# Renumbered weight slots and new step lists in a graph transformer and GAT kernel

## The chip, the cores and the metric

The kernel runs on one core of a Trainium2 chip. A core has a matrix engine (PE, with its weight loader PEld), a vector engine (DVE), a scalar engine (ACT), a general engine (POOL) and a queue engine (SP) that here issues nearly all DMAs. Each engine works through its own instructions in the order in which the program gives them; between engines semaphores order the work. The metric is the time of the whole kernel on the device in microseconds (us), lower being better.

## The reference, cut to what matters

The input is `x` of 128 graphs x 128 nodes x 512 features, and a weighted adjacency `adj` of 128 x 128 x 128. Two layers follow each other, each with a layer norm and a relu in front and a residual sum behind:

```python
h = jnp.maximum(_layernorm(x, axis=-1), 0.0)
q, k, v = (h @ W.T + b for W, b in ((Wq, bq), (Wk, bk), (Wv, bv)))   # 8 heads of 64
scores = q @ k.T * SCALE * (adj + adj)        # per head
x = x + softmax(scores) @ v @ Wo.T + bo
h = jnp.maximum(_layernorm(x, axis=-1), 0.0)
Wh = h @ W
e = leaky_relu(Wh @ a[:512] + (Wh @ a[512:]).T, 0.2)
x = x + elu(softmax(where(adj > 0.5, e, -9e15), axis=1) @ Wh)
```

Everything is float32.

## The kernel before, in words

**Units of work.** Two graphs are a pair (64 pairs, `p`), two pairs are a group (32 groups, `g`). A group's query, key and value projections are not computed as plain products. The 4 x 4 blocks of the three weight matrices and the 4 blocks of tokens and features go through a fast matrix multiplication scheme: 26 block products (`TERMS`), 17 sums of input blocks per group (`FORMS`), and 35 sums of weight blocks that are computed once (`WSUMS`). The other two large products, of the attention context with `Wo` and of the gathered features with `W`, take 7 block products per pair (`PRODUCTS`).

**Steps and names.** The kernel is cut into small steps, each with a short name and a pair:

- `Tk` makes form `k` on POOL (L281). `Qn` multiplies term `n` for queries and keys (L296, two matmuls that the profile records as four passes of 256 columns), `Vn` for values (L305, four passes of 128 columns). `An` and `Bn` take the accumulated sum out of PSUM after the term: the first for a block is a copy by ACT (L320, L333), the others are additions by DVE (L322, L335). Terms of one chain go on accumulating in the same bank, so the next product of the chain has to wait until the take has read it.
- `sca`, `scb` are the attention scores of the pair's two graphs (PE L373), `at..` weighs them with the adjacency (DVE L380), `mx.` takes the maxima (DVE L387), `ex..` the exponentials (ACT L392), `rc..` the reciprocals (DVE L396), `nm..` scales (ACT L401).
- `fl.` transposes 32 x 32 blocks (DVE L408), `bl.` writes them to DRAM (SP L412), `pl.` reads them back into transposed places (SP L418, four DMAs), and `pc.` multiplies with the values (PE L441). `pe.` and `cs0` to `cs3` prepare the context for the seven products (ACT L448, DVE L190 to L196).
- `o0` to `o6` are the seven products with `Wo` (PE L348), `od..` adds them to `x` (DVE L455). `w0` to `w6` are those with `W` (PE L348), `zc.` copies and `wd.` adds their results (ACT L548, DVE L552). `g0`, `g1` gather (PE L534).
- `lx`, `l0`, `lT`, `la`, `lt`, `f0` are loads on SP; `t0`, `t1` (DVE L204, L205) take layer norm statistics of the pair five further on, `pp` (POOL L212) their power, `hn` normalises (DVE L229), `tp` transposes on PE (L236), `ev` keeps the transposed rows (ACT L239): the first four pairs are normalised in this way.
- `L0` to `L3` load four raw weight blocks each into `w_sb` (SP L160, 768 KB each), `W0` to `W34` are the sums of weight blocks (DVE L166, L169).

**Order.** Nothing is scheduled at run time, and PE, DVE, ACT, POOL and SP each take their share of the steps in the order of three written lists. `HEAD` (730 entries `step@pair`) is run once. `ORDER` (341 entries `step:lag`, acting on pair `2g - lag`) is run for `g` from 2 to 28, so 27 times; each turn does one group's worth of every step. `TAIL` (1051 entries, the number counted back from the last pair) ends the work. A name that stands where no such step exists any more is passed over. All PSUM tiles come in turn from one pool of 8 banks (`ps1`).

**Buffers near the change.** `w_sb` has 28 slots of three 128 x 128 blocks. Slots 0 to 15 take the raw blocks, and many of the sums overwrite raw blocks that are used up. The host lays `wT` out so that it matches the slots.

Of the kernel before, what the change touches and what calls it, by code (L numbers as in the profile page):

```python
# [13 lines left out]
P = 128  # L14
# [10 lines left out]
def kernel(  # L25
# [16 lines left out]
    nc = tc.nc  # L42
    B, S, E = x.shape
    C = E // P
# [22 lines left out]
    def sums(text):  # L67
# [7 lines left out]
        1,8,7,13- 0,10,18,10- 1,9,19,03- 0,11,0,00- 1,1,20,01+ 0,2,16,. 1,13,5,11+ 0,0,21,03- 1,12,6,12- 0,0,1,02-  # L75
        1,14,14,02- 0,18,24,00+ 0,3,26,01+ 3,20,15,03+ 2,21,22,02- 3,19,25,13+ 2,22,23,12- 3,16,9,11- 2,6,10,.
        3,17,27,01- 2,4,2,13+ 3,15,4,00- 2,4,3,10- 3,23,12,10- 2,24,8,12+ 2,7,13,11-
# [5 lines left out]
        7=15-7 16=8-4 17=15-11 18=17-16 0=1-0 19=7-18 19=19-0 9=9n11 11=9n15 5=5-11 20=5-7 6=6n5 5=14n6 21=15-3  # L83
        21=21-0 22=10n17 23=1n2 24=23-22 25=24-15 3=3+1 1=25+3 14=14n22 24=12n24 26=13-12 27=11-12 2=7+2 2=3+2 4=11-4
        3=3n19 17=8-17 12=17-12 8=19+20 8=5-8 11=5+11 13=11-13
# [55 lines left out]
    w_sb = const.tile([P, SLOTS, 3, P], F32, name="w3")  # L141
# [16 lines left out]
    def load_blocks(n):  # L158

        nc.sync.dma_start(w_sb[:, n : C * C : C], wT[:, n : C * C : C])  # L160
# [464 lines left out]
    def listed(text, mark):  # L625
# [3 lines left out]
        lx@1 t0@-4 t1@-4 lx@0 t0@-5 pp@1 hn1@1 tp1@1 ev1@1 hn0@1 L0@0 L3@0 W2@0 W0@0 t1@-5 pp@0 W1@0 lx@2 t1@-3 tp0@1  # L629
        ev0@1 T0@-2 hn1@0 tp1@0 ev1@0 T4@-2 T8@-2 L1@0 W7@0 hn0@0 W4@0 W3@0 V0@-2 B0@-2 tp0@0 ev0@0 W8@0 W5@0 W13@0  # L630
        W9@0 Q0@-2 A0@-2 W6@0 T1@-2 Q2@-2 T2@-2 V1@-2 l0@-2 t0@-2 L2@0 t1@-2 V2@-2 T3@-2 B1@-2 V3@-2 B3@-2 B2@-2
        W14@0 Lu@0 W10@0 pp@3 hn0@3 Q1@-2 A1@-2 la@-1 W16@0 W11@0 V5@-2 V7@-2 B7@-2 Q3@-2 A2@-2 Q4@-2 V4@-2 A3@-2
        W15@0 hn1@3 W17@0 W19@0 W12@0 W18@0 W21@0 B4@-2 W20@0 W29@0 W31@0 Q5@-2 Q7@-2 A7@-2 W22@0 Lo1@0 W24@0 A4@-2
        T5@-2 Q6@-2 V6@-2 tp1@3 A6@-2 Q8@-2 Q9@-2 B6@-2 V8@-2 A8@-2 W25@0 V9@-2 Lc@0 l0@0 t1@0 T7@-2 t0@-3 t0@0 T9@-2
        T10@-2 A9@-2 Q11@-2 A11@-2 ev1@3 B9@-2 W23@0 V11@-2 tp0@3 T6@-2 Q10@-2 B8@-2 ev0@3 W26@0 W28@0 T11@-2 T12@-2
        Q13@-2 s0@0 A13@-2 A10@-2 V10@-2 Q12@-2 W27@0 W33@0 Q15@-2 A15@-2 A12@-2 B10@-2 T13@-2 V14@-2 Q14@-2 V13@-2
        B13@-2 B11@-2 A14@-2 Q17@-2 A17@-2 B14@-2 pp@2 V15@-2 V12@-2 B15@-2 T16@-2 T14@-2 Q16@-2 A16@-2 hn1@2 V16@-2
        B16@-2 Q19@-2 A19@-2 Q18@-2 Q20@-2 l0@-1 t1@-1 Q21@-2 V18@-2 V17@-2 A20@-2 hn0@2 A21@-2 W30@0 B17@-2 Q22@-2
        A22@-2 B12@-2 W32@0 T0@0 t0@-1 Q0@0 T15@-2 V20@-2 Q23@-2 A23@-2 sca@0 Lo0@0 Wo0@0 Lw0@0 scb@0 ata1@0 ata0@0
        Q24@-2 A0@0 tp0@2 ev0@2 V0@0 B20@-2 V22@-2 mxa@0 exa3@0 exa2@0 W34@0 tp1@2 l0@2 la@0 B22@-2 V24@-2 V19@-2  # L640
# [299 lines left out]
```

## Time and profile before

| what | value |
|---|---|
| time of the kernel, median of three runs | 2327.14 us (2325.97 to 2329.51) |
| the profiled execution's own time | 2323.18 us |
| its span, first to last instruction | 2321.4 us |
| mean granted PE clock | 0.997 |
| PE busy, share of the span | 2291.4 us, 99% |
| DVE busy | 2099.9 us, 90% |
| ACT busy | 1460.3 us, 63% |
| POOL busy | 972.8 us, 42% |
| 16 DMA engines, mean busy share | about half; 0.93 in the first 20 us |
| PE busy in the first 200 us | 184.99 us |
| PE busy in the last 200 us | 187.31 us |

One turn of `ORDER` takes 70.95 us in the middle of the run: the same burst of score products begins at 1033.61 and again at 1104.55. So the 27 turns make up 1915.7 us of the span; the remaining 406 us belong to `HEAD` and `TAIL`. In the middle of the run a stretch of 73 us has 72.93 us of busy PE and about 66.4 us of busy DVE. A busy PE is not yet a PE at its fastest, because the profile models where a matmul ends: what counts is the distance from one start to the next. The profiler's times of one execution are used below for single instructions, the median of the runs for the kernel.

### The profile page before, as it was taken

Reading aid. Unit: us, or ns where it says so; the run is one execution under the profiler, and the core shown is the slowest. Engines: PE = TensorE matmul, PEld = TensorE weight load, DVE = VectorE, ACT = ScalarE, POOL = GpSimd, SP = SyncE. Lnnn points to the kernel's source line nnn. Section 1 sums busy time; section 2 is a strip of 40 time slices with the busy share of each in tenths; the row PEclk is TensorE's granted clock in tenths of the full one; section 3 lists DMA queues with packets and bytes.
Section 4 is the critical chain, followed back from the end, with each engine's and each line's share of the span. In section 5 each row is a group of like instructions: output and inputs, shape, how many; then the busy total and the mean of one; then the engine's idle time right before and its main releaser. Section 6 shows DMA issues by size and latency. Waiting matters only on the chain.

```text
span 2321.4 us, 45352 instructions
## 1 busy us (share of the span) xinstructions
PE 2291.4 (99%) x15444; PEld 2037.5 (88%) x15444; DVE 2099.9 (90%) x4620; ACT 1460.3 (63%) x4942; POOL 972.8 (42%) x1112
## 2 busy tenths in 40 slices
PE   8999999999999999999999999999999999999998
PEld 6888888888888888888888888888888888888986
DVE  8998999998999999999989999999999899999897
ACT  2566666666665766666666657666666666566665
POOL 3634443443443444434434434444344344344211
PEclk9999999999999999999999999999999999999999
DMA  4544654545544545545455455454454554544432
GB/s 164 148 119 119 157 137 135 148 120 145 151 124 138 144 121 157 135 137 148 120 145 150 124 139 139 125 157 134 137 143 126 145 150 124 139 125 124 119 121 89
DMA packets 267471, 314.60 MB, mean 136 GB/s; under 512 B 23656, under 2 KB 193640, under 8 KB 267240
## 3 DMA queue, kind: packets, MB, share of 16 engines
q1 hardware_dynamic: 263736, 311.57, 48.6%
q8 instruction: 123, 2.02, 0.4%
q0 software_dynamic: 1920, 0.13, 0.1%
q14 instruction: 108, 0.88, 0.1%
q10 hardware_dynamic: 1584, 0.01, 0.0%
HBM read 210.77 MB, written 100.85 MB: 134 GB/s over the span
## 4 chain that ended last, share of the span: by engine, by line
PE 92%; DVE 4%; DMA 1%; ACT 1%; issue 1%; POOL 1%; SPq 0%; POOLq 0%; DVEq 0%; ACTq 0%
PE acc_q L296 30%; PE row_a L348 24%; PE acc_v L305 14%; PE row_c L348 9%; PE pc L441 5%; PE sc L373 5%; PE pg L534 5%; DVE st L204 1%; DVE w L169 1%; DVE qk L322 1%; ACT z L548 1%; DMA aT<-blocks 0%; DMA w<-in_wT 0%; DVE junk L478 0%; DVE x L455 0%
## 5 line engine op out<-in xcount | busy, mean ns | idle before, releaser
L296 PE MATMUL acc_q<-tf,w 128*128 128x256 f32 x2176 | 550.1, 384 | 2.2 <-DVE w L169 1.6
L281 POOL TENSOR_TENSOR tf<-hA,tf 128x256 f32<-128x256 f32 x288 | 225.0, 786 | 660.7 <-PE acc_v L305 642.4
L296 PEld LDWEIGHTS acc_q<-tf,w 128*128 128x128 f32 x2176 | 393.0, 190 | 63.0 <-ACT qk L320 8.4
L392 ACT ACTIVATE at<-at,nmx 128x128 f32<-128x128 f32 x1024 | 397.5, 391 | 35.8 <-DVE nmx L387 33.7
L322 DVE TENSOR_TENSOR qk<-qk,acc_q 128x512 f32<-128x512 f32 x512 | 341.8, 678 | 31.6 <-PE acc_q L296 28.4
L305 PEld LDWEIGHTS acc_v<-w,tf 128*128 128x128 f32 x2176 | 312.4, 191 | 24.7 <-POOL tf L281 2.1
L348 PE MATMUL row_a<-w,gT 128*128 128x256 f32 x1272 | 327.7, 384 | 4.3 <-ACT gT L540 0.7
L401 ACT ACTIVATE at<-at,rs 128x128 f32<-128x128 f32 x1024 | 329.1, 396 | 1.2 <-DVE rs L396 1.2
L305 PE MATMUL acc_v<-w,tf 128*128 128x128 f32 x2176 | 321.6, 275 | 1.9 <-POOL tf L281 1.8
L348 PE MATMUL row_a<-wo,cxT 128*128 128x256 f32 x1272 | 320.9, 382 | 0.8 <-DVE x L455 0.5
L296 PE MATMUL acc_q<-hA,w 128*128 128x256 f32 x1152 | 295.3, 380 | 0.0
L348 PEld LDWEIGHTS row_a<-w,gT 128*128 128x128 f32 x1272 | 233.6, 190 | 42.3 <-ACT z L548 8.5
L348 PEld LDWEIGHTS row_a<-wo,cxT 128*128 128x128 f32 x1272 | 231.5, 190 | 37.3 <-DVE x L455 10.0
L335 DVE TENSOR_TENSOR v<-v,acc_v 128x256 f32<-128x256 f32 x512 | 206.2, 408 | 33.1 <-PE acc_v L305 31.7
L296 PEld LDWEIGHTS acc_q<-hA,w 128*128 128x128 f32 x1152 | 208.7, 190 | 27.3 <-DVE qk L322 4.3
L380 DVE SCALAR_TENSOR_TENSOR at<-sc,adj 128x512 f32<-128x512 f32 x256 | 166.1, 681 | 44.3 <-PE sc L373 44.2
L478 DVE SCALAR_TENSOR_TENSOR junk<-h,u 128x512 f32<-128x512 f32 x256 | 200.2, 782 | 3.4 <-ACT h L471 1.0
L281 POOL TENSOR_TENSOR tf<-hA 128x256 f32<-128x256 f32 x128 | 93.4, 741 | 257.8 <-PE acc_v L305 194.0
L548 ACT COPY z<-row_a 128x256 f32<-128x256 f32 x256 | 93.3, 364 | 163.3 <-PE row_a L348 158.6
L392 ACT ACTIVATION_READ_ACCUMULATOR at<-at,nmx 128x1 f32 x1024 | 194.0, 189 | 0.0
L320 ACT ACTIVATE qk<-acc_q,bq 128x256 f32<-128x256 f32 x256 | 120.1, 469 | 113.7 <-PE acc_q L296 113.6
L269 POOL TENSOR_TENSOR x<-x,c 128x512 f32<-128x512 f32 x128 | 174.9, 1386 | 22.5 <-DMA x<-in_x 9.5
(97 smaller groups left out, 4162.8 us busy)
## 6 DMA issues: line engine op xcount, KB each, us to landing
blocks<-tr SPq DMA_DIRECT2D x128, 512.0 KB, 5.5
aT<-blocks SPq DMA_DIRECT2D x512, 128.0 KB, 3.5
x<-in_x SPq DMA_DIRECT2D x123, 512.0 KB, 4.0
out<-x SPq DMA_DIRECT2D x63, 512.0 KB, 3.3
hA<-in_xT SPq DMA_DIRECT2D x120, 256.0 KB, 4.1
mr<-rows SPq DMA_DIRECT2D x60, 256.0 KB, 3.2
adj<-in_adj SPq DMA_DIRECT2D x64, 128.0 KB, 2.2
adjT<-in_adjT SPq DMA_DIRECT2D x64, 128.0 KB, 5.5
```

The lines of the kernel that those rows point to most:

```text
L269: nc.gpsimd.tensor_tensor(xs[p][:, i, :], xs[p][:, i, :], c_sb, OP.add)
L281: eng.tensor_tensor(forms[g, 2 * C + k], form(g, a), form(g, b), OP.add if op == "+" else OP.subtract)
L296: nc.tensor.matmul(acc[:, i, :], w_sb[:, slot, i, :], form(g, f), start=fresh and i == 0, stop=True, skip_group_check=True)
L305: nc.tensor.matmul(acc[:, i, :], form(g, f)[:, i * P : (i + 1) * P], w_sb[:, slot, 2, :], start=fresh and i == 0, stop=True, skip_group_ch ...
L320: nc.scalar.activation(d[:, i, :], acc[:, i, :], AF.Identity, bias=bias[:, j : j + 1], scale=float(sign))
L322: nc.vector.tensor_tensor(d, d, acc, OP.add if sign > 0 else OP.subtract)
L335: nc.vector.tensor_tensor(d, d, acc, OP.add if sign > 0 else OP.subtract)
L348: nc.tensor.matmul(acc, left[:, la, c, :], w[:, wb, c, :], start=first, stop=c == 1, skip_group_check=True)
L380: nc.vector.scalar_tensor_tensor(ats[b][0][:, k * C : (k + 1) * C, :], scs[b][k], QSCALE, adjs[p][:, i : i + 1, :].to_broadcast([P, C, S]) ...
L392: nc.scalar.activation(at[:, j, :], at[:, j, :], AF.Exp, bias=nmx[:, j : j + 1], accum_out=sums[:, j : j + 1])
L401: nc.scalar.activation(at[:, j, :], at[:, j, :], AF.Copy, scale=rs[:, j : j + 1])
L478: nc.vector.scalar_tensor_tensor(junk, h2[:, i, :], 1.0, u_sb[:, k, :], op0=OP.mult, op1=OP.mult, accum_out=ws[:, i, 1:2] if k else src_sb ...
```

## The change

The change renumbers slots and rewrites lists; no instruction's shape and no arithmetic is changed.

- `wT` is laid out on the host by output block and then by input block, where it was the other way round, so that the four blocks that one `load_blocks` brings stand next to each other, in DRAM as well as in `w_sb`. Each of the four loads then moves 6,144 bytes per partition in one run where it moved four runs of 1,536 bytes. `TERMS` and `WSUMS` name the new slot numbers; the sums and products are the same.
- `HEAD`, `ORDER` and `TAIL` hold the same steps in another order. The cut between the three lists is moved too (710, 341 and 1071 entries): a few steps that ended `HEAD` now begin `ORDER`.

The core of the diff, with the beginning of `HEAD`, and of `ORDER` the lines that matter later:

```diff
     TERMS = list(terms("""
-        1,8,7,13- 0,10,18,10- 1,9,19,03- 0,11,0,00- 1,1,20,01+ 0,2,16,. 1,13,5,11+ 0,0,21,03- 1,12,6,12- 0,0,1,02-
+        1,8,13,13- 0,10,18,10- 1,9,19,03- 0,11,0,00- 1,1,20,01+ 0,2,16,. 1,13,5,11+ 0,0,21,03- 1,12,9,12- 0,0,4,02-
...
     WSUMS = list(sums("""
-        7=15-7 16=8-4 17=15-11 18=17-16 0=1-0 19=7-18 19=19-0 9=9n11 11=9n15 5=5-11 20=5-7 6=6n5 5=14n6 21=15-3
+        13=15-13 16=2-1 17=15-14 18=17-16 0=4-0 19=13-18 19=19-0 6=6n14 14=6n15 5=5-14 20=5-13 9=9n5 5=11n9 21=15-12
...
-        nc.sync.dma_start(w_sb[:, n : C * C : C], wT[:, n : C * C : C])
+        nc.sync.dma_start(w_sb[:, n * C : (n + 1) * C], wT[:, n * C : (n + 1) * C])
...
     HEAD = """
-        lx@1 t0@-4 t1@-4 lx@0 t0@-5 pp@1 hn1@1 tp1@1 ev1@1 hn0@1 L0@0 L3@0 W2@0 W0@0 t1@-5 pp@0 W1@0 lx@2 t1@-3 tp0@1
-        ev0@1 T0@-2 hn1@0 tp1@0 ev1@0 T4@-2 T8@-2 L1@0 W7@0 hn0@0 W4@0 W3@0 V0@-2 B0@-2 tp0@0 ev0@0 W8@0 W5@0 W13@0
-        W9@0 Q0@-2 A0@-2 W6@0 T1@-2 Q2@-2 T2@-2 V1@-2 l0@-2 t0@-2 L2@0 t1@-2 V2@-2 T3@-2 B1@-2 V3@-2 B3@-2 B2@-2
...
+        lx@1 t0@-4 L3@0 t1@-4 lx@0 t0@-5 L1@0 pp@1 hn0@1 hn1@1 W2@0 t1@-5 W13@0 tp0@1 ev0@1 W7@0 W0@0 tp1@1 L0@0
+        ev1@1 pp@0 hn1@0 tp1@0 ev1@0 W1@0 T0@-2 V0@-2 hn0@0 tp0@0 W8@0 W3@0 W4@0 T4@-2 B0@-2 ev0@0 W5@0 T1@-2 T2@-2
+        W9@0 Q0@-2 A0@-2 W6@0 V2@-2 T3@-2 B2@-2 Q2@-2 V1@-2 B1@-2 Q1@-2 l0@-2 t1@-2 t0@-2 pp@3 A2@-2 T5@-2 V3@-2 lx@2
...
     ORDER = """
...
-        sca:0 scb:0 pea:1 peb:1 pw:2 nm:2 h20:2 h21:2 ata0:0 w0:3 zc0:3 ata1:0 V25:2 cs0:1 mxa:0 exa1:0 exa0:0 d10:2
-        d00:2 atb1:0 px:2 rca0:0 atb0:0 w2:3 T1:0 Q2:0 zc2:3 T3:0 T2:0 f0:0 Q1:0 V1:0 exa2:0 T7:0 t0:-2 nma0:0 w4:3
-        mxb:0 A2:0 nma1:0 exb0:0 o0:1 B25:2 zc4:3 lx:1 sh:1 o1:1 od0:1 w3:3 V0:0 exb1:0 cs1:1 o2:1 B1:0 t1:-2 lT:0
-        exa3:0 d11:2 T5:0 Q4:0 exb3:0 od1:1 wd4c:3 rcb0:0 od2:1 w1:3 cs2:1 rca1:0 lT:-1 cs3:1 wd1:3 pd:2 d01:2 pv:2
-        hd0:0 hd1:0 exb2:0 rcb1:0 A1:0 wm:2 l0:-1 nma3:0 nma2:0 o4:1 o3:1 w6:3 od4:1 V3:0 Q3:0 f0:-1 fla:0 bla:0
...
-        V5:0 la:-2 lt:0 blb:0 od6:1 B2:0 V4:0 pr:2 m1:2 B4:0 A6:0 e1:2 V7:0 s0:-2 T6:0 T9:0 B7:0 od5:1 Q7:0 A7:0
-        hd0:-1 Q8:0 st0:1 Q9:0 sw:2 A9:0 V6:0 pla:0 V9:0 B9:0 g1:2 st1:1 hd1:-1 zc5:3 fa:3 T10:0 V11:0 g0:2 B6:0 V8:0
-        B11:0 Q11:0 A11:0 ge1:2 ez:3 gs0:2 B8:0 V10:0 B10:0 T11:0 T12:0 fb:3 A8:0 Q10:0 plb:0 Q13:0 A13:0 so:3 lx:0
-        gs2:2 pw:1 nm:1 h21:1 h20:1 V12:0 A10:0 gs1:2 B12:0 Q12:0 A12:0 Q15:0 A15:0 pca:0 sca:-1 scb:-1 pcb:0 ata1:-1
...
+        pr:3 A20:2 V18:2 V20:2 B20:2 V21:2 B21:2 od4:2 wd6:4 m1:3 o3:2 Q22:2 Q0:0 fa:4 o5:2 A22:2 e1:3 sw:3 T16:2
+        V22:2 B22:2 Q24:2 ez:4 A0:0 T15:2 Q23:2 T8:0 od4c:2 o6:2 V23:2 V24:2 T1:0 pla:1 od1:2 A24:2 od5:2 fb:4 g1:3
+        ge1:3 g0:3 plb:1 ge0:3 od6:2 B24:2 st0:2 st1:2 Q25:2 A25:2 gs2:3 B23:2 gs0:3 so:4 V25:2 B25:2 A23:2 pca:1
+        pcb:1 sca:0 scb:0 T2:0 pw:2 nm:2 peb:1 cs0:1 h21:2 ata0:0 ata1:0 h20:2 d10:2 mxa:0 pea:1 d00:2 Q2:0 atb1:0
+        atb0:0 A2:0 Q1:0 V1:0 o0:1 o1:1 exa2:0 A1:0 w0:3 w1:3 lt:1 lT:0 V0:0 T3:0 T5:0 px:2 cs1:1 lt:2 cs2:1 Q4:0
+        Q3:0 mxb:0 lx:1 sh:1 od0:1 o2:1 exa1:0 exa3:0 f0:0 hd0:0 T7:0 rca1:0 t0:-2 exa0:0 exb3:0 zc0:3 B0:0 V2:0
+        t1:-2 B1:0 V3:0 rca0:0 od1:1 A3:0 Q5:0 nma0:0 od2:1 cs3:1 o4:1 Q7:0 o3:1 hd1:0 B2:0 pd:2 pv:2 B3:0 wd1:3
+        nma1:0 gs1:3 w2:3 d01:2 od4:1 l0:-1 la:-2 exb2:0 A4:0 gs3:3 wm:2 d11:2 rcb1:0 nma2:0 zc2:3 V4:0 nma3:0 fla:0
+        lT:-1 t1:-1 od4c:1 w3:3 f0:-1 o5:1 w4:3 V5:0 V7:0 exb0:0 B4:0 V6:0 pr:2 nmb2:0 m1:2 od5:1 A7:0 hd0:-1 B7:0
+        exb1:0 rcb0:0 T9:0 T6:0 st0:1 B6:0 bla:0 nmb3:0 zc4:3 wd4c:3 Q6:0 o6:1 od6:1 nmb1:0 nmb0:0 A6:0 T10:0 Q9:0
+        V9:0 V8:0 flb:0 e1:2 A9:0 st1:1 w6:3 wd6:3 blb:0 Q8:0 hd1:-1 w5:3 sw:2 B8:0 B9:0 V11:0 A8:0 pla:0 Q11:0 V10:0
+        T11:0 T12:0 zc5:3 fa:3 A11:0 B11:0 plb:0 g0:2 g1:2 ez:3 ge1:2 fb:3 so:3 pw:1 nm:1 B10:0 V13:0 ge0:2 h21:1
+        Q13:0 A13:0 gs0:2 V12:0 gs2:2 Q12:0 Q15:0 gs1:2 Q10:0 B12:0 h20:1 d10:1 A10:0 A12:0 gs3:2 d00:1 pca:0 sca:-1
+        scb:-1 pcb:0 peb:0 ata1:-1 pea:0 ata0:-1 B13:0 px:1 pd:1 mxa:-1 atb1:-1 w0:2 zc0:2 atb0:-1 exa1:-1 T14:0
+        T13:0 V14:0 exa3:-1 exa2:-1 exa0:-1 V15:0 B15:0 A15:0 mxb:-1 exb2:-1 w1:2 exb0:-1 o0:0 lx:0 exb3:-1 cs0:0
...
-            np.transpose(np.reshape(np.stack([L0_gnn_Wq, L0_gnn_Wk, L0_gnn_Wv]), (3, 4, P, 4, P)), (4, 3, 1, 0, 2)),
+            np.transpose(np.reshape(np.stack([L0_gnn_Wq, L0_gnn_Wk, L0_gnn_Wv]), (3, 4, P, 4, P)), (4, 1, 3, 0, 2)),
```

## The prediction

> **What bounds the kernel now.** I read first the busy shares and slices of the page, then the chain of work that ended last over one turn of the loop, then the order of PE's instructions in time around the breaks of that chain, then the waits by engine, and last the first 24 us.
>
> ```profile
> PE 2291.4 (99%) x15444; PEld 2037.5 (88%) x15444; DVE 2099.9 (90%) x4620; ACT 1460.3 (63%) x4942; POOL 972.8 (42%) x1112
> PE   8999999999999999999999999999999999999998
> ```
>
> PE is busy throughout, but its ends are modelled. The chain gives its pace, in start us, us, what:
>
> ```profile
> 1031.71 1.90 PE pc L441 x32
> 1033.61 1.99 PE sc L373 x32
> 1040.47 2.59 PE row_a L348 x12
> 1055.78 1.34 PE acc_v L305 x12
> 1068.84 1.02 PE pc L441 x16
> ```
>
> A pass of 256 columns costs 2.59/12 = 0.216 us, one of 128 columns 1.34/12 = 0.112. A turn has 26 Q steps and 14 products with Wo and W per pair, (26 + 28) x 4 = 216 wide passes, 46.6 us; 104 passes of V and 32 of g, 136 narrow ones, 15.2; two bursts of scores, 3.98; contexts 1.90 + 2 x 1.02 = 3.94. Sum 69.7 us. Going in and out of a burst of scores and contexts costs about 0.1 us each time, 0.4 in a turn. A turn takes 70.95. So about 0.8 us of a turn is PE standing, and it is here:
>
> ```profile
> 1036.49 0.61 PE L305 MATMUL acc_v<-w,hA 128*128 128x128 f32 x4
> 1037.17 1.13 PE L348 MATMUL row_a<-w,gT 128*128 128x256 f32 x4
> ...
> 1056.95 1.03 PE L296 MATMUL acc_q<-hA,w 128*128 128x256 f32 x4
> 1057.88 1.13 PE L296 MATMUL acc_q<-tf,w 128*128 128x256 f32 x4
> ```
>
> These are PE's rows: start, length, line, operation. V25's four passes begin at 1036.49 and take 4 x 0.112; w2 begins at 1037.17, 0.24 late. And a group of four wide passes that runs through has 1.03 us, one that follows a wait has 1.13: each wait costs 0.10 us on top of itself. The waits of the whole run name the producers (total us, times, longest):
>
> ```profile
> PEld row_a L348 <- DVE x L455: 10.0, 31, 0.9
> PEld row_a L348 <- ACT z L548: 8.5, 30, 0.9
> PEld acc_q L296 <- ACT qk L320: 8.4, 29, 0.3
> PEld acc_q L296 <- DVE qk L322: 5.1, 29, 0.5
> ```
>
> About 30 times means once in each turn. From the rows in time the five places are, late plus 0.10: w2 after zc0 0.24 + 0.10 (1037.17); o4 after od2 0.05 + 0.10 (1046.85); Q8 after A6 0.06 + 0.10 (1057.88); Q9 after A7 0.02 (1058.84); Q10 after A8 0.06 + 0.10 (1064.67). Sum 0.83, which is the 0.8 (two of the five are shown above, the others read in the same rows). The loop is thus 98.8% PE at its own pace; DVE with 66.4 of 73 us has room.
>
> The head is different. PE in the first 24 us, and the chain there:
>
> ```profile
> 8.17 1.11 PE L236 MATMUL pt<-ident,hn 128*128 128x128 f32 x8 [1.35 <-DVE hn L229]
> 15.28 1.11 PE L236 MATMUL pt<-ident,hn 128*128 128x128 f32 x4 [6.00 <-DVE hn L229]
> 18.05 1.91 PE L296 MATMUL acc_q<-tf,w 128*128 128x256 f32 x4
> 21.57 1.10 PE L296 MATMUL acc_q<-tf,w 128*128 128x256 f32 x4 [1.61 <-DVE w L169]
> ```
>
> ```profile
> 4.40 6.77 DMA w<-in_wT
> 11.19 1.03 DVE w L169 x2
> ```
>
> PE stands for 6 us until pair 0 is normalised on DVE, which itself stands 2.6 us for a load of weights and then sums weights. PE is busy for 185.0 of the first 200 us and 187.3 of the last 200.
>
> **What the Trainium skill says.** "TensorE: Matmul & The Clock Gate", Architectural detail: PE can pull weight loads ahead of running matmuls, while ACT and DVE are strict first in, first out. The trace agrees: without a wait the loads are hidden (0.216 a pass, while a load lasts 0.19), and a take of PSUM is late when something long stands before it on its engine. The page has no price for a restart; the 0.10 is this trace's. Same page, What's actually happening: after about 3.4 us idle PE runs at half clock, and as long again until it recovers. The trace agrees: after the 6 us gap Q0's four passes take 1.91 us, later ones 1.10. "DMA: Bandwidth & Descriptors", Why small descriptors are slow: about 3 cycles a packet beside 32 bytes a cycle. For four runs of 1,536 bytes against one of 6,144 that is 204 against 195 cycles, 4%.
>
> **The change, part by part.** Durations come from the profiled execution (2323.18 us; span 2321.4, and 1.8 around it). The median of the runs is 2327.14, 4.0 more, which I carry over unchanged.
>
> *Contiguous loads.* Same four DMAs, same bytes. At 324 GB/s (the first 20 us) 768 KB take 2.4 us; 4% of it, an estimate from that page, is 0.1 us a load. Bounds: 0 to 0.5 us for all four; I take 0.2, inside the head's figure below. Slot numbers cost nothing: same instructions, same shapes.
>
> *ORDER, the five waits.* Each goes if enough PE work stands between the take's source and the product that waits. (Q, o or w = 0.86 us, V = 0.45, g = 0.89.)
> - w2 behind zc0: between w0 and w2 stood V25 (0.45), and it was 0.24 late, so 0.69 is needed. For lag 3 twelve steps now stand there. For lag 2 the waiting one is now w1, with V14 and V15, 0.90, between: margin 0.2.
> - Q9 behind A7: only Q8 stood between Q7 and Q9; now eleven steps.
> - Q8 behind A6: A6 stood in ACT's queue behind pr (two instructions) and nmb; now two nmb steps, four scalings of about 0.3 us by their spacing, and o6, Q9, V9, V8, w6 (3.5 us) cover them.
> - Q10 behind A8: A8 stood behind ge1 and ez, and Q10 next to it. Now g0, g1, V13, Q13, V12, Q12, Q15 and more lie between, over 5 us.
> - o4 behind od2: Q4 and w1 (1.72) lay between o2 and o4, and on DVE d11 (1.0), od1, wd4c and a reciprocal went ahead of od2. Now V2, V3 and Q5 (1.76) lie between; the statistics t0 and t1 that go ahead on DVE need no product and can run during Q4 and Q3, so that od1 and od2 (0.4 each) are what is left after o2: margin near 0.8.
>
> So the 0.83 goes. New tight places in the new list: Q24 behind A22 has Q0, o5 and V22 (2.17 us), while DVE has fa (1.2) and A22 (0.7) to do, margin 0.3; the margin of w1 is 0.2; Q15 behind A13 has V12 and Q12 as before. If one of these is late by 0.05 it costs 0.15 a turn. Bounds: none late (0) to two late by 0.1 (0.4). I take 0.15. The bursts (pca pcb sca scb, and pca sca scb pcb) stand as before, so their 0.4 stays. A stall that goes moves PE forward only; DVE then has about 64.5 us of work in a 70.3 us turn, so nothing new is full. Net 0.8 - 0.15 = 0.65 a turn, times 27 = 17.6 us; from 0.4 x 27 = 11 to 0.83 x 27 = 22.
>
> *HEAD.* L3 is now issued ahead of x of pair 0, so W2 no longer waits until 11.19. But in DVE's queue t0@-5 (x of pair 0) stands ahead of hn0@1, and 768 KB more in front of it, 2.4 us at 324 GB/s, put it near 8.7 instead of 6.56. From there, by the rows of DVE before: statistics to 9.6, two hn to 10.5, W2 11.0, statistics 11.9, W13, W7, W0 to 13.4, hn1@0 there. Before, hn1@0 began at 14.62. V0, 1.6 behind it, thus begins near 15.0 where it was 16.18, gain 1.2. Then W5 and T1 are ready about when Q0 ends; Q2 had stood 1.6 us for a weight sum after Q0, so 1 to 2 more may go. From 20 to 80 us DVE is 98% busy (58.6 of 60), so the lead holds only as far as DVE is ahead, and DVE's idle time shrinks by no more than 1 to 2. Later breaks, such as the 1.8 us for V11@0 on POOL near 78 us, may go or come. I take 3 us; 0 to 7.
>
> *TAIL.* In the last 36 us the order of products and DVE work is nearly the same, and in the 70 us before the same work remains at each mark within 2 us. I take 1; -3 to 3.
>
> Sum: 17.6 + 3 + 1 = 21.6; profiled execution 2301.6, median 2327.1 - 21.6 = 2305.5.
>
> **Rivals.**
> 1. *The waits are moved, not removed* (0.18). ACT and DVE take in order, and some take of the new list is late by 0.2 or more in each turn. For: 26 takes and products are packed as tightly as before. Against: the worked margins. Half of the loop's gain goes: 0.35 x 27 = 9.5, and 2 of the head: 2315.
> 2. *The change does nothing measurable* (0.06): the new head is late on x of pair 0 and the loop's gain is eaten by new waits of 0.7 a turn: 2325 to 2329.
> 3. *Slower: the round trip of the attention blocks comes late* (0.07). flb's blocks are written (median landing 5.5 us) and read back (3.5) before pcb. Before, 8 Q, 8 V, 2 g steps and the burst's 3.0 lay between blb and pcb: 15.3 us. Now Q8, w5, V11, Q11, V10, g0, g1, V13, Q13, V12, Q12, Q15, Q10 and 3.0: 12.6 us. The trip needs 9.0 by the medians, 12.7 by the longest ones of the run (6.6 and 6.1). It decides from 3.6 us of extra delay. Late by 1.5 + 0.1 in each turn, against 0.65 gained: 0.95 x 27 = 26, less 3 of the head: 2350. Against: PE waited for these blocks only twice, 2.4 us in all.
> 4. *The head gives more* (0.04): 7 us and a clean loop of 0.83: 2327 - 30 = 2297.
>
> **The numbers.** The forecast has 0.65, and its own range is 2297 to 2312 (loop 11 to 22, head and tail together 0 to 8, not all at their ends at once). Rival 1 fills 2312 to 2320. The range 2295 to 2320 leaves out rivals 2 and 3 and a little at both ends. A difference under 0.2% (4.7 us) can't be told from none here. Faster: 0.65 + 0.18 + 0.04 = 0.87; same 0.06; slower 0.07.
>
> **What would show it.** Right: a turn of 70.1 to 70.5 us between equal bursts; the four PEld rows above with few or no counts of 29 to 31; no wide group of 1.13 us outside the bursts' ends; V0 near 15; DVE's wait for the weight load gone and one for x in its place. Wrong: a PE wait of about 27 counts with a longest over 0.2, above all for A22, zc0 or the blocks read back; a turn over 70.7; or PE busy under 185 of the first 200 us.

## The result and the profile after

The changed kernel takes 2298.41 us (median of four runs, 2295.39 to 2298.97), the kernel before beside it 2328.32 (2325.97 to 2329.70). The ratio is 0.9873, 95% interval 0.9859 to 0.9888, so 26 to 33 us faster; 21.6 had been forecast. The profiled execution took 2298.78 us, its span is 2297.0. The first lines of the page:

```profile
span 2297.0 us, 45596 instructions
PE 2271.0 (99%) x15444; PEld 2041.3 (89%) x15444; DVE 2083.2 (91%) x4620; ACT 1456.8 (63%) x4942; POOL 925.4 (40%) x1112
```

PE runs the same 15,444 products. Its share of the span was 99% and is 99%, although 24.4 us of span are gone: the busy time fell by 20.4 us with it. That is because the profile counts a pass to its modelled end and lets a pass slowed by a wait count as busy. The share says nothing here; the distance between equal places does. The bursts of attention scores in the chain (start in us, length, what):

```profile
1059.86 1.02 PE pc L441 x16
1060.88 1.99 PE sc L373 x32
1062.87 1.02 PE pc L441 x16
...
1129.97 1.02 PE pc L441 x16
1130.99 1.99 PE sc L373 x32
```

A turn now takes 1130.99 - 1060.88 = 70.11 us; it took 70.95. That is 0.84 a turn and 22.7 us in 27 turns. Between these rows the chain goes from product to product and never leaves PE. The waits of the whole run (total us, times, longest) say the same:

```profile
PEld pc L441 <- issue: 10.6, 32, 0.3
PEld sc L373 <- DVE v L335: 4.6, 27, 0.2
...
PEld row_a L348 <- DVE w L492: 4.6, 27, 0.2
...
PE pc L441 <- DMA aT<-blocks: 2.0, 2, 1.2
...
PEld row_a L348 <- ACT z L548: 1.6, 4, 0.9
...
PEld acc_q L296 <- DVE qk L322: 1.0, 4, 0.3
```

The four rows that had 29 to 31 counts have 3 or 4, or are gone. What still has 27 to 32 counts are short weight loads at the edges of the bursts, the same places as before. No new row took the place of the old ones, and PE waited for the blocks read back only twice.

The head is another matter. Rows of PE there (start, length, and in brackets how long it stood and for whom):

```profile
10.89 1.97 PE L236 MATMUL pt<-ident,hn 128*128 128x128 f32 x8 [5.07 <-DVE hn L229]
15.09 1.12 PE L236 MATMUL pt<-ident,hn 128*128 128x128 f32 x4 [2.23 <-DVE hn L229]
16.00 1.06 PE L305 MATMUL acc_v<-w,tf 128*128 128x128 f32 x4
...
19.94 0.71 PE L305 MATMUL acc_v<-w,tf 128*128 128x128 f32 x4 [0.92 <-DVE st L204]
...
133.00 1.13 PE L348 MATMUL row_a<-wo,cxT 128*128 128x256 f32 x4 [1.95 <-DVE cxT L196]
133.96 0.71 PE L305 MATMUL acc_v<-w,hA 128*128 128x128 f32 x4
134.47 1.91 PE L296 MATMUL acc_q<-hA,w 128*128 128x256 f32 x4
136.17 1.81 PE L296 MATMUL acc_q<-tf,w 128*128 128x256 f32 x4
```

V0, the first product of acc_v, begins at 16.00 where it began at 16.18; about 15.0 was forecast. And at 133 us there is something that no step of the forecast had: PE waits 2 us, and then two groups of four passes take 1.9 us each instead of 1.03. DVE's rows of the same stretch, and that of the load at 9 us:

```profile
9.28 0.69 DVE L204 BATCH_NORM_STATS2 st<-x 128x6 f32<-128x512 f32 x1 [2.97 <-DMA x<-in_x]
...
129.68 1.87 DVE L508 SCALAR_TENSOR_TENSOR w<-adjT,w 128x256 f32<-128x256 f32 x1
...
132.53 0.41 DVE L196 TENSOR_TENSOR cxT<-pc,cxT 128x256 f32<-128x256 f32 x1
```

The mask's product wm (L508), 0.4 us elsewhere, has 1.87 here: its transfer pv was issued at 126.38, and wm follows pv directly in the new HEAD. Behind it in DVE's queue stands cs3 (L196), for which PE waits.

To compare heads whose orders differ, I use PE's idle time up to a stage: the start of the stage, less the passes that PE had done by then, each at the pace of the loop (the warm-up passes at the very start are left out). For the scores of pair 3 that is 147.28 - 119.34 = 27.94 us before and 149.19 - 119.79 = 29.40 after. By these two traces the new head loses 1.5 us. The experiments had to say whether that is so, where the remaining gain lies (29.9 measured, 24.4 between the profiled executions), and whether the five waits of the loop are the whole of its story.

### The profile page after: what moved, and what is told of

Same layout as the page of the kernel before. It is cut to its first block, busy times and chain, and to the rows that moved or that the text cites. A ratio compares the mean times of both kernels' runs of the same rounds, so it can differ in the third digit from the quotient of the medians.

```text
span 2297.0 us, 45596 instructions
## 1 busy us (share of the span) xinstructions
PE 2271.0 (99%) x15444; PEld 2041.3 (89%) x15444; DVE 2083.2 (91%) x4620; ACT 1456.8 (63%) x4942; POOL 925.4 (40%) x1112
## 4 chain that ended last, share of the span: by engine, by line
PE 94%; DVE 3%; DMA 2%; SPq 0%; issue 0%; POOL 0%; ACT 0%; POOLq 0%; DVEq 0%
PE acc_q L296 30%; PE row_a L348 24%; PE acc_v L305 15%; PE row_c L348 9%; PE pc L441 5%; PE sc L373 5%; PE pg L534 5%; DMA x<-in_x 1%; DMA aT<-blocks 0%; DVE st L204 0%; DMA adj<-in_adj 0%; DMA c<-in_bo 0%; DVE w L169 0%; DVE at L380 0%; DVE hn L229 0%
## 5 line engine op out<-in xcount | busy, mean ns | idle before, releaser
L296 PE MATMUL acc_q<-tf,w 128*128 128x256 f32 x2176 | 539.9, 382 | 1.3 <-POOL tf L281 0.9
L401 ACT ACTIVATE at<-at,rs 128x128 f32<-128x128 f32 x1024 | 334.5, 392 | 33.5 <-DVE rs L396 33.4
L305 PEld LDWEIGHTS acc_v<-w,tf 128*128 128x128 f32 x2176 | 304.9, 192 | 20.8 <-POOL tf L281 2.3
L269 POOL TENSOR_TENSOR x<-x,c 128x512 f32<-128x512 f32 x128 | 160.6, 1276 | 245.6 <-DMA x<-in_x 165.7
L262 POOL TENSOR_TENSOR hA<-hA,mr 128x512 f32<-128x512 f32 x120 | 153.9, 1304 | 183.1 <-DMA mr<-rows 183.1
L448 ACT COPY cxT<-pc 128x512 f32<-128x512 f32 x128 | 71.5, 582 | 245.4 <-PE pc L441 245.4
L540 ACT COPY gT<-pg 128x512 f32<-128x512 f32 x128 | 72.0, 586 | 209.9 <-PE pg L534 209.9
L408 DVE STREAM_TRANSPOSE tr<-at 128x1024 f32<-128x1024 f32 x128 | 158.3, 1237 | 33.6 <-ACT at L401 33.6
L204 DVE BATCH_NORM_STATS2 st<-x 128x6 f32<-128x512 f32 x256 | 173.0, 676 | 10.5 <-DMA x<-in_x 8.3
```

The source lines that it names most:

```text
L204: nc.vector.bn_stats(st, src[:, i, :])
L262: nc.gpsimd.tensor_tensor(h[:, c : c + 2], h[:, c : c + 2], row[:, c : c + 2], OP.subtract)
L269: nc.gpsimd.tensor_tensor(xs[p][:, i, :], xs[p][:, i, :], c_sb, OP.add)
L296: nc.tensor.matmul(acc[:, i, :], w_sb[:, slot, i, :], form(g, f), start=fresh and i == 0, stop=True, skip_group_check=True)
L305: nc.tensor.matmul(acc[:, i, :], form(g, f)[:, i * P : (i + 1) * P], w_sb[:, slot, 2, :], start=fresh and i == 0, stop=True, skip_group_ch ...
L401: nc.scalar.activation(at[:, j, :], at[:, j, :], AF.Copy, scale=rs[:, j : j + 1])
```

## The experiments

Each kernel was run on the same chip as runs of the kernel before, whose medians there were 2327.2 (25 runs, 2322.78 to 2331.72), 2327.6, 2326.2 and 2326.8 us. The profiled execution of before, 2323.18, thus lies at the lower edge of its own runs. The changed kernel has two medians, 2298.41 and, in a repetition below, 2296.60. The repetition, the moves with their eviction, and the last two kernels ran on one chip. The old head, the wait put back, x ahead of the weights and the mask later ran on another. The medians of the kernel before lie 1.4 us apart from chip to chip, so there a difference of about 1 us from the changed kernel says little.

### The loads alone

The lists stay as before; slots, `TERMS`, `WSUMS` and the layout are new:

```diff
-        nc.sync.dma_start(w_sb[:, n : C * C : C], wT[:, n : C * C : C])
+        nc.sync.dma_start(w_sb[:, n * C : (n + 1) * C], wT[:, n * C : (n + 1) * C])
```

> The three old lists of steps with the new numbers of the raw slots and the contiguous loads: the loads alone. Theory (the loads are worth 0.1 us each at the head, and PE does not wait for them): 0 to 0.5 us faster than before, so same. Rival (the loads carry part of the gain, or of the 5 us by which the measured gain exceeds the gain of the two profiled executions): 1 to 6 us faster, and V0 or the head's later stages earlier by that much.

Measured 2327.03 us (13 runs), ratio 1.0001, interval 0.9993 to 1.0009: no difference that can be seen. V0 begins at 16.18 us, as before, and the load whose landing the profile has takes 6.8 us from issue to landing in both traces. So no worth of the contiguous loads can be measured, as forecast, and the gain comes from the lists.

The run showed something else. With the very same HEAD, its profiled execution has 32.42 us of idle time at the scores of pair 3, where before's has 27.94. The biggest part is one wait. PE there, in this kernel:

```profile
77.67 1.16 PE L373 MATMUL sc<-qk 64*128 64x128 f32 x16
81.75 0.71 PE L305 MATMUL acc_v<-w,tf 128*128 128x128 f32 x4 [2.91 <-POOL tf L281]
82.29 4.87 PE L583 MATMUL pm<-wo,bv 128*128 128x256 f32 x14
```

and in the kernel before:

```profile
76.72 1.16 PE L373 MATMUL sc<-qk 64*128 64x128 f32 x16
79.67 0.71 PE L305 MATMUL acc_v<-w,tf 128*128 128x128 f32 x4 [1.78 <-POOL tf L281]
80.22 2.97 PE L583 MATMUL pm<-wo,bv 128*128 128x256 f32 x13
```

V11 of pair 0 waits for the sums that POOL makes, 2.91 or 1.78 us, and after the longer wait the next 14 passes take 4.87 us. Most of them start 0.43 us apart instead of 0.216: half the clock. POOL was late because it waited for a load of row statistics (L262, its bracket):

```profile
71.50 2.54 POOL L262 TENSOR_TENSOR hA<-hA,mr 128x512 f32<-128x512 f32 x2 [3.93 <-DMA mr<-rows]
```

In before's trace the same row begins at 69.40 after 2.77 us. So the old head varies from execution to execution. Seven traces in all were taken with the old HEAD, and at the scores of pair 3 they have 27.9, 29.5, 29.6, 30.0, 30.2, 30.7 and 32.4 us of idle time: before's own is the lowest, the mean is 30.1. What part of this is the clock is worked out below, with the second trace of the changed kernel.

### The loop alone

Old numbers, layout and HEAD, new ORDER; HEAD gets five steps more at its end, and TAIL is the new one's first 59 entries and then what is left of the old one:

```diff
     HEAD = """
...
+        B17@2 V19@2 B19@2 s0@3 T4@4
     """
     ORDER = """
-        w6:4 Q22:2 o4:2 blb:1 pr:3 m1:3 wd6:4
+        fla:1 bla:1 w4:4 zc4:4 od2:2 Q18:2 w3:4
...
```

> The old numbers, loads and HEAD (with five steps added at its end so that the new ORDER finds what it needs), the new ORDER, and a TAIL that joins the two: the loop alone. Theory (the gain is the loop's, 27 turns by 0.84 us, and the new HEAD gave back 1.4 us): turn 70.1 us as in the changed kernel, 21 to 25 us faster than before, and no slower than the changed kernel. Rival (head and tail carry 7 us or more of the 30 measured): at most 20 us faster.

2303.90 us (2303.20 to 2308.51), ratio 0.9904 (0.9889 to 0.9919): 19 to 26 us faster, and its turn is 1063.78 - 993.66 = 70.12 us. So the loop carries 22 to 23 us of the gain, as the theory says. But it is 5.5 to 7.3 us slower than the two medians of the changed kernel, and "no slower" was wrong. The trace shows three places: 2.3 us where HEAD meets ORDER (32.74 us of idle time at the scores of pair 4 after 30.03 at pair 3; other kernels add 0.45 there), 1.6 us after PE's last product (6.6 us to the end of the span against 5.0), and the rest in the head itself.

### The old head on the new kernel

The reverse: everything new but HEAD, and the same five steps at its end:

```diff
     HEAD = """
-        lx@1 t0@-4 L3@0 t1@-4 lx@0 t0@-5 L1@0 pp@1
+        lx@1 t0@-4 t1@-4 lx@0 t0@-5 pp@1 hn1@1 tp1@1
...
+        B17@2 V19@2 B19@2 s0@3 T4@4
     """
```

> The changed kernel with the old HEAD (and the five steps that join it to the new ORDER); numbers of the slots, loads, ORDER and TAIL are the new ones. Theory (the new HEAD reaches the scores of pair 3 1.4 us later than the old one in the profiled executions): 0.7 to 2.5 us faster than the changed kernel. Rival (the new HEAD is a gain, as forecast, and the two profiles differ by chance): 1 to 4 us slower than the changed kernel.

2302.41 us (2301.82 to 2302.69), ratio 0.9891 (0.9876 to 0.9905): 4 to 6 us slower than the changed kernel. The theory was wrong, and the sign is the rival's. The size is not a measure of the old HEAD, though: again 2.7 us come between pairs 3 and 4 (29.58 to 32.28), which is the seam that I made. The HEAD itself has 29.58 at pair 3.

### The changed kernel again

Nothing is edited here.

> The changed kernel once more, for a second trace of its head beside those of the other kernels, and a time of the same call. Theory (its HEAD repeats within 1 us, while the old HEAD, in six traces so far, had PE idle between 27.9 and 32.4 us up to the scores of pair 3, before's own profiled execution being the lowest): 28.9 to 29.9 us idle at that point, median 2296 to 2299. Rival (the new HEAD varies as much): idle outside 28.5 to 31.

2296.60 us (2295.61 to 2298.39), and 26.50 us of idle time at the scores of pair 3 instead of 29.40. So the rival is right here too: the new HEAD varies as well. The wait at 130 us is there again (1.80 us), but this time the passes after it run at full clock. The clock records of the traces show why. They grant full or half clock in pieces of 3.41 us or whole multiples of it, the last piece of a run apart, and what decides is how busy PE was in the window of 3.41 us just before. First the changed kernel's first trace, then this one (start and end, length, PE busy, weight loads, DVE, ACT and POOL busy, PE clock, DMA share, GB/s):

```profile
130.92:134.33 3.41, 1.46 (x9) 1.23 (x9) 3.41 (x10) 2.66 (x8) 1.14 (x2) 1.00 0.05 15
134.33:137.75 3.42, 3.42 (x11) 2.79 (x10) 3.11 (x6) 1.26 (x5) 0.00 (x0) 0.50 0.63 200
```

```profile
129.26:132.67 3.41, 1.78 (x9) 1.25 (x8) 3.41 (x10) 2.21 (x7) 1.59 (x3) 1.00 0.24 29
132.67:136.09 3.42, 3.42 (x21) 3.08 (x20) 3.42 (x7) 2.67 (x9) 0.85 (x2) 1.00 0.55 141
```

With 1.46 us of busy PE the next window has half the clock, with 1.78 us it keeps full clock. In all 14 traces of this document it is the same: each of the 38 windows at full clock with up to 1.59 us of busy PE was followed by half clock, and none of the other 9,332, with 1.63 us or more. So the same wait costs more or less by how it falls on these windows. A window of busy PE at half clock loses 1.7 us. From 140 us to the end of the loop no trace has one, so the turns compared here are free of it.

Three traces with the new HEAD (the first, that of the wait put back, below, and this one) have 29.4, 29.0 and 26.5, mean 28.3. Against 30.1 of the old HEAD that is 1.8 us less, not 1.5 more. But beyond the 10.24 us at half clock that the head begins with, the seven traces of the old HEAD have eight windows at half clock and the three of the new one have one. At 1.7 us each (an estimate) that is 1.4 of the 1.8 us. One trace of each kernel was not enough to judge such a head, and three against seven, which spread by 2.9 and 4.5 us, don't prove the 1.8.

### One wait of the loop taken away

The kernel before, w2 moved behind Q2:

```diff
-        rca0:0 atb0:0 w2:3 T1:0 Q2:0 zc2:3 T3:0
+        rca0:0 atb0:0 T1:0 Q2:0 w2:3 zc2:3 T3:0
```

> The kernel before with one step moved in ORDER: w2 behind Q2, so that the eight passes of Q2 stand between zc0 and the wait of w2. Theory (a wait of PE costs the time waited, 0.24 us, and a slow first pass after it, 0.10 us): 0.34 us a turn, 9.2 us faster. Rivals: only the time waited counts, 6.5 us faster; the wait moves to the next pass that needs DVE or ACT, 0 to 2 us.

2319.26 us (2317.15 to 2320.61), ratio 0.9964 (0.9951 to 0.9976), 6 to 11 us faster. The turn is 1067.06 - 996.45 = 70.61, 0.34 less than before, to the hundredth what the wait of 0.24 and its slow pass of 0.10 make; 27 times that is 9.2. PE's rows behind the burst:

```profile
1033.06 1.13 PE L348 MATMUL row_a<-w,gT 128*128 128x256 f32 x4
...
1034.47 1.03 PE L296 MATMUL acc_q<-tf,w 128*128 128x256 f32 x4
1035.34 1.03 PE L348 MATMUL row_a<-w,gT 128*128 128x256 f32 x4
```

w2 (the last row) has 1.03 and starts when Q2 ends. Only w0 behind the burst still has 1.13. The wait neither moved on nor cost only its length. It is the turn that shows this: the interval of the time holds the 6.5 us of the first rival too.

### All five waits taken away by hand

Each of the five places gets one more row of products ahead of the wait:

```diff
-        w2:3 T1:0 Q2:0
+        T1:0 Q2:0 w2:3
...
-        o4:1 o3:1 w6:3
+        w6:3 o4:1 o3:1
...
-        Q8:0 st0:1 Q9:0 sw:2 A9:0 V6:0 pla:0 V9:0 B9:0
+        V6:0 Q8:0 st0:1 V9:0 Q9:0 sw:2 A9:0 pla:0 B9:0
...
-        V10:0 B10:0 T11:0 T12:0 fb:3 A8:0 Q10:0
+        V10:0 V12:0 B10:0 T11:0 T12:0 fb:3 A8:0 Q10:0
```

> The kernel before with five steps moved in ORDER, so that each of the five rows of acc or row passes that stood behind a late helper gets one more row ahead of it (w2 behind Q2, V6 and V9 ahead of Q8 and Q9, V12 behind V10, w6 ahead of o4): no new search. Theory (the loop loses 0.83 us a turn in these five waits and nowhere else): all five go, turn 70.1 to 70.3, 18 to 22 us faster than before. Rival (a wait that is taken away in one place comes back at the next, as the engines behind it are no faster): turn 70.6 or more, under 10 us faster.

2327.06 us (13 runs), ratio 0.9996 (0.9988 to 1.0005): nothing at all. The turn is 1249.99 - 1179.05 = 70.94. All five waits are gone, and two others have come, of the same sum: V11 is 0.57 + 0.07 late, Q15 0.08 + 0.10. PE and then ACT at V11 (PE's bracket counts from the modelled end of the pass before, 0.57 is from start to start):

```profile
1205.39 1.05 PE L534 MATMUL pg<-w,h 128*128 128x128 f32 x8
1206.85 0.68 PE L305 MATMUL acc_v<-w,tf 128*128 128x128 f32 x4 [0.40 <-ACT v L333]
```

```profile
1205.60 0.47 ACT L320 ACTIVATE qk<-acc_q,bq 128x256 f32<-128x256 f32 x1 [2.06 <-DVE st L204]
1205.97 0.47 ACT L320 ACTIVATE qk<-acc_q,bk 128x256 f32<-128x256 f32 x1
1206.32 0.39 ACT L333 ACTIVATE v<-acc_v 128x256 f32<-128x256 f32 x1
```

V11 needs the bank that ACT empties with `v<-acc_v` (B9, at 1206.32). V9 was now done before Q9, but B9 still stood behind A9, the taking of Q9, in ACT's queue. The Trainium skill, "TensorE: Matmul & The Clock Gate", Architectural detail, calls ACT's queue strictly first in, first out, and this trace agrees: ACT stood 2.06 us with B9 waiting behind. (The profile names a DVE statistic as what ended ACT's wait. A9 doesn't read that; it reads Q9, whose passes run from 1204.53 and end at about the same moment.)

### The moves with their eviction

The same, with B9 moved ahead of A9 along with V9, and V12 left in its place:

```diff
-        Q8:0 st0:1 Q9:0 sw:2 A9:0 V6:0 pla:0 V9:0 B9:0
+        V6:0 Q8:0 st0:1 V9:0 Q9:0 sw:2 B9:0 A9:0 pla:0
```

> The kernel before with w2 behind Q2, w6 ahead of o4, V6 ahead of Q8, and V9 together with its eviction B9 ahead of Q9 and A9; V12 stays. In the run of five moves V9 went ahead of Q9 but B9 stayed behind A9 in ACT's queue, and V11, which needs the buffer that B9 frees, waited 0.57 us. Theory (that order of ACT's queue was the cause): the wait of V11 goes, four of the five waits stay away (0.34 + 0.15 + 0.16 + 0.02 = 0.67 us a turn), turn 70.3, 16 to 19 us faster than before. Rival (the V passes are wanted ahead of V11, whatever the order of evictions): V11 waits on, turn 70.7 to 70.9.

2309.72 us (2305.93 to 2316.70), ratio 0.9934 (0.9920 to 0.9947): 12 to 19 us faster. The turn is 1064.82 - 994.51 = 70.31, so 0.64 less. PE at V11 again:

```profile
1196.16 1.05 PE L534 MATMUL pg<-w,h 128*128 128x128 f32 x8
1197.06 0.61 PE L305 MATMUL acc_v<-w,tf 128*128 128x128 f32 x4
1197.50 1.06 PE L534 MATMUL pg<-w,h 128*128 128x128 f32 x8
```

V11 follows without a wait. One wait is left, Q10 behind A8 with 0.09 + 0.10, which this kernel doesn't touch. So four short moves and one eviction give three quarters of what the new loop gives. Two things differ from the run of five moves. V12 is back in its place, which takes Q15's 0.18 away and brings Q10's 0.19 back; B9's place in ACT's queue takes V11's 0.64 away. The order of ACT's queue decided between three quarters and nothing.

The six runs spread by 11 us, and the granted clock on record with each goes with it: 2305.93 us at a mean of 0.998, 2309.08 to 2309.85 at 0.996, 2313.14 at 0.994 and 2316.70 at 0.993.

### A wait put back

The changed kernel, w1 moved to right behind V14, so that V14's 0.45 us alone cover zc0:

```diff
-        V14:0 exa3:-1 exa2:-1 exa0:-1 V15:0 B15:0 A15:0 mxb:-1 exb2:-1 w1:2
+        V14:0 w1:2 exa3:-1 exa2:-1 exa0:-1 V15:0 B15:0 A15:0 mxb:-1 exb2:-1
```

> The changed kernel with one step moved in ORDER: w1 of one pair right behind V14, so that only V14's four passes stand between it and w0 and zc0's chain is no longer covered in full. Theory (a wait put into the loop costs its length and a slow pass of 0.10 us): one wait of about 0.2 to 0.3 us comes back each turn, turn 70.4 to 70.5, 7 to 11 us slower than the changed kernel. Rival (the loop has slack elsewhere that takes it up): turn 70.1, within 2 us.

2308.55 us (2308.43 to 2308.83), 10 to 12 us slower than the two medians of the changed kernel. The turn is 1065.34 - 994.82 = 70.52, 0.41 more, times 27 = 11.1. A row of the list of waits is back with the size it had before the change:

```profile
PEld row_a L348 <- ACT z L548: 8.8, 31, 0.9
```

w1 is 0.24 + 0.10 late, and 0.07 come at the next Q. The loop has no slack that would take up even a quarter of a microsecond.

### x ahead of the weights

The changed kernel, L3 behind the x of pair 0 in HEAD:

```diff
-        lx@1 t0@-4 L3@0 t1@-4 lx@0 t0@-5 L1@0
+        lx@1 t0@-4 t1@-4 lx@0 L3@0 t0@-5 L1@0
```

> The changed kernel with one step moved in HEAD: the load of the projection weights (L3 of pair 0) behind the x of pair 0 rather than ahead of it. Theory (x of pair 0 came 0.6 us later than forecast because the weights' 64 KB go ahead of it in the same queues, and V0 waits for x and not for the weights): DVE's 2.97 us wait for x shrinks to under 1.5, V0 1 to 1.6 us earlier, 0.5 to 1.6 us faster than the changed kernel. Rival (the weights are then late for the evictions ev, as they were in the kernel before): V0 no earlier, 0 to 1 us slower.

DVE's rows for x of pair 0 and for the first sum of weights, and PE's V0:

```profile
6.70 0.69 DVE L204 BATCH_NORM_STATS2 st<-x 128x6 f32<-128x512 f32 x1 [0.34 <-DMA x<-in_x]
...
9.63 0.56 DVE L169 TENSOR_TENSOR w<-w 128x384 f32<-128x384 f32 x1 [0.92 <-DMA w<-in_wT]
```

```profile
14.43 1.06 PE L305 MATMUL acc_v<-w,tf 128*128 128x128 f32 x4
```

x is there 2.6 us earlier, the weights cost 0.92, and V0 begins 1.57 us earlier. The time is 2296.63 us (2295.04 to 2296.96), 1.8 under the changed kernel's first median and equal to its second, so the theory holds in the trace and the time can't tell it. (The 64 KB of the expectation is a slip: L3 brings 768 KB.)

### The mask later

The changed kernel, wm of pair 0 moved from right behind pv to behind d01:

```diff
-        hd0@2 hd1@2 pv@0 wm@0 rcb0@2
+        hd0@2 hd1@2 pv@0 rcb0@2
...
-        d11@0 fla@2 bla@2 d01@0 A4@2
+        d11@0 fla@2 bla@2 d01@0 wm@0 A4@2
```

> The changed kernel with one step moved in HEAD: the mask's product wm of pair 0 from right behind pv, whose transfer it needs, to behind d01, 20 steps on. Theory (wm held DVE for 1.87 us, cs3 behind it was late, PE waited 2.1 us for it and then ran about eight passes at half the clock): the wait of 2.1 us at the passes o5 of pair 1 goes with the slow passes after it, 3 to 4 us faster than the changed kernel. Rivals: the load of x for pair 3 (l0, t1) is late by itself, and the wait stays within 1 us, under 1.5 us faster; or the wait goes but the half clock has another cause, some 2 us faster.

2294.85 us (2294.14 to 2296.12). PE at o5 of pair 1, where it stood 1.95 us:

```profile
131.38 1.13 PE L348 MATMUL row_a<-wo,cxT 128*128 128x256 f32 x4 [0.29 <-DVE cxT L196]
132.35 0.61 PE L305 MATMUL acc_v<-w,hA 128*128 128x128 f32 x4
132.79 1.03 PE L296 MATMUL acc_q<-hA,w 128*128 128x256 f32 x4
```

The wait is down to 0.29, the slow passes are gone, and at pair 3 the idle time is 26.28 us against 26.5 to 29.4. Gain 1.8 to 3.6 us by the two medians; 3 to 4 was expected of a wait with half the clock after it, which, as the second trace showed, is not always there.

### Both, and one step further

Both moves in HEAD together:

```diff
-        lx@1 t0@-4 L3@0 t1@-4 lx@0 t0@-5 L1@0
+        lx@1 t0@-4 t1@-4 lx@0 L3@0 t0@-5 L1@0
...
-        hd0@2 hd1@2 pv@0 wm@0 rcb0@2
+        hd0@2 hd1@2 pv@0 rcb0@2
...
-        d11@0 fla@2 bla@2 d01@0 A4@2
+        d11@0 fla@2 bla@2 d01@0 wm@0 A4@2
```

> The changed kernel with both moves in HEAD: x of pair 0 ahead of the weights, and the mask's product behind d01. Theory (the two losses lie at 9 us and at 130 us, with nothing between that would take one of them up: 1.6 and 3.1 us less idle time of PE at the scores of pair 3, each alone): 4 to 5.5 us faster than the changed kernel, about 2293.5. Rival (PE's wait at o5 of pair 1 is for the load of x of pair 3 by then, which does not move with the start): 3 to 3.5 us, no better than the mask's move alone.

2293.32 us (2291.59 to 2294.54), ratio 0.9856 (0.9842 to 0.9871). All four runs are faster than each of the eight runs of the changed kernel (2295.39 to 2298.97); this version beats both kernels. Its gain is 3.3 us against the changed kernel on the same chip and 5.1 against the first median. The first is where the rival had it, the second where the theory had it, so the time doesn't decide between them. In the trace the idle time at the scores of pair 3 is 25.3 us, 1.0 less than with the mask's move alone: by one trace of each, some of the 1.6 us of x is kept.

The last kernel has both moves, and POOL's statistics of pair 2 (s0) go from ahead of the sums T7 to T12 of pair 0 to behind them:

```diff
-        Q9@0 s0@2 A8@0 Q10@0 hd1@0 T7@0 T9@0 T10@0 T11@0 T12@0
+        Q9@0 A8@0 Q10@0 hd1@0 T7@0 T9@0 T10@0 T11@0 T12@0 s0@2
```

> The kernel with both moves in HEAD, and one more: s0 of pair 2 (POOL's two operations on the row statistics and the issue of their transfer, 2.55 us in the changed kernel from the end of hd0 to the start of T7) from ahead of T7 of pair 0 to behind T12. Theory (PE waits for the sums T that POOL makes, 0.33 us at V11 and 1.06 us at Q13 of pair 0, because s0 stands ahead of them): both waits go, 1 to 1.4 us faster than with both moves, about 2292. Rival (PE then waits at V9 or Q13 for DVE's evictions instead, or the later statistics hold up pair 2): 0 to 0.5 us.

2295.85 us (2293.70 to 2298.02): no gain over the two moves. V11's wait of 0.33 us went, Q13's fell from 1.06 to 0.60, but Q14 now waits 0.88 for a sum, and pcb of pair 0, 0.83 late in the kernel with both moves, stood much longer (its row in PE's timeline):

```profile
94.28 1.70 PE L441 MATMUL pc<-aT,v 128*64 128x128 f32 x16 [2.54 <-DVE w L180]
```

The profile names a DVE sum as what ended this wait, but pcb doesn't read that sum. The blocks that it does read, the last of them issued by 86.3, took 8.2 us from issue to landing in the median of that stretch, against 5.8. The wait also left PE busy for only 0.87 us of a window, and the next 3.41 us ran at half clock. Whether the moved statistics caused that or it was this one execution stays open; the theory's gain, at any rate, did not come.

## Why the prediction was right

The forecast of 2305.5 us, range 2295 to 2320, holds the 2298.4; the sign and the cause were right, and the gain was 8 us short of the medians. By traces that share a part, it adds up so (idle time of PE):

| stage | forecast | traces |
|---|---|---|
| head, to the scores of pair 3 | 3 | 30.1 - 28.3 = 1.8 (seven and three traces; not clear of their spread) |
| loop, pair 3 to pair 63 | 17.6 | 42.8 - 19.3 = 23.5 (before and after) |
| end, pair 63 to PE's last w6 | 1 | 12.08 - 10.14 = 1.9 (five and three traces) |
| after PE's last product | none | 6.2 - 5.0 = 1.2 |
| sum | 21.6 | 28.4 |

- *The five waits go.* Right, and shown: 0.84 a turn against 0.83 read from the rows. One of them alone was worth 0.34, as worked out, and one put back cost 0.41.
- *New waits of 0.15 a turn.* Wrong. None came: Q24 behind A22 and w1 behind zc0, with margins of 0.3 and 0.2, hold in all turns. This is the term that was mis-sized most: 27 x 0.15 = 4 of the 7 us that the sums differ by. But the caution had its reason: the five moves made by hand took the same five waits away and lost all of it again.
- *Loads.* Right: 0.2 us was allowed, nothing was measured. (204 against 195 cycles is 4.6%, not 4%, and between w0 and w2 of lag 3 stand eleven products, not twelve; neither matters.)
- *Head.* The order of events was right and each time late: x at 9.28 (forecast near 8.7, though 6.56 and 2.4 make 8.96), hn1@0 at 14.08 (13.4), V0 at 16.00 (near 15.0). Late x alone is 0.6 of that: moved ahead of the weights it came 2.6 earlier, and V0 1.6. The breaks that were said to "go or come" did both: V11's wait of 1.8 to 3.0 us became 0.3 there and 1.1 at Q13, and the wait at o5 behind wm, 1.8 to 2.6 us, is new. For this the forecast followed every step to 20 us and none beyond; the pair pv and wm, next to each other in HEAD, could have been seen in the list.
- *End.* 1 us was forecast; 1.9, and 1.2 more after the last product, were found. What of TAIL makes them was not tried.
- *The median taken 4.0 above the profiled execution, unchanged.* For the changed kernel it is not so: its profiled execution, 2298.78, lies among its runs. Before's profiled execution was a short one: it has no window at half clock in the head beyond the first 10.24 us, and the other six traces of the old HEAD have one to three, at 1.7 us each. The runs say the same. Of the 50 runs of the kernel before beside the experiments, the 12 with a mean granted clock of 0.997, as in the profiled execution, took 2324.7 us on average, the 24 with 0.996 took 2327.2, the 11 with 0.995 took 2328.0 and the three below that 2331.4.

Rival 1, waits moved and not removed, is false for this change and true for the five moves by hand. Rival 2 is false. Rival 3, the round trip of the blocks, is false: PE waited for them twice. Rival 4 named nearly the time, 2297, with a clean loop, which came, and 7 us from the head, which didn't; that the time came so near is partly luck, since the end, which it left out, gave 3.1. Of the signs for "wrong", one came up by a hair: PE is busy for 184.78 of the first 200 us, against 184.99. It was a poor sign: the kernel before is itself under the 185 that it names, and passes at half the clock count as busy.

## What to carry to other kernels

When one engine is busy 99% of the time, measure the distance between equal places in the loop, and price every wait as its length plus the slow pass that follows. Moving a product means moving the evictions that empty its bank, in the queue of the engine that does them; otherwise the wait comes back one product on. Before a head that waits for transfers is judged, look at several traces of it and at the clock granted in each: one trace of each kernel had the new head 1.5 us behind, where the means of several have it 1.8 ahead, most of which is the clock.

## What was not expected of the hardware

- A wait of PE costs about 0.10 us beyond its length. Ahead of wide passes the second comes 0.320 us after the first instead of 0.216; ahead of narrow ones the extra is 0.07 to 0.10, and waits as short as 0.05 and 0.06 us (ahead of o4 and Q8) have it too. A wait of 0.24 taken out of 27 turns moved the turn by 0.34.
- Waits of 2 to 3 us sometimes bring the half clock and sometimes don't: after 2.1 (changed kernel), 2.6 (x ahead of the weights) and 2.97 us (loads alone) the passes ran at half pace, after 2.64 (the wait put back) and 2.66 (one wait taken away) they did not. The Trainium skill, "TensorE: Matmul & The Clock Gate", What's actually happening, has a window of about 3.4 us that runs freely and isn't tied to the kernel, and the pieces of 3.41 us in the clock records agree. The page speaks of an idle window; here a window need not be idle. Up to 1.59 us of busy PE in it brought the half clock, from 1.63 us on it did not come. The wait of 2.64 us fell on two windows, with 2.35 and 2.00 us of busy PE, and the one of 2.1 us left 1.46 us in a single one. In the head of the kernel before, from which the prediction read the half clock, the clock fell at 10.35 us, early in the 6 us gap, after a window with 1.11 us of busy PE. (Busy times are the profile's, with modelled ends.)
- The way back has such a border too: of the 63 full windows at half clock in the 14 traces, those with up to 2.64 us of busy PE were followed by another at half clock, those with 2.79 us or more by full clock.
- A transfer of 2 KB of statistics, written and read back in 256 KB to all partitions, made POOL wait for 2.77 us in one execution and for 3.93 in another of the same head, and PE's own wait, for POOL's sums, grew from 1.78 to 2.91 us.
